# Products of ones ahead of the transposes of norms, two transposes handed on, and keys ahead of relative products, in a decoder kernel of twelve sublayers

## The chip, the cores and the metric

The kernel runs on one core of one Trainium2 chip. The metric is the device time of one execution in microseconds (us); lower is better. The engines are TensorE (PE in the profile, its weight loads PEld), VectorE (DVE), ScalarE (ACT), GpSimd (POOL) and SyncE (SP, which here only issues DMAs). Everything that TensorE multiplies lands in PSUM, eight banks of 128x512 float32 values, and another engine has to take it from there.

## The reference, cut to what matters

A decoder of four layers works on x of 16 sequences x 64 tokens x 128 features. Each layer has three sublayers, and each sublayer ends in the same way:

```
x = layernorm(x + sublayer(x), axis=-1)      # twelve times
```

In order: linear attention (called `la` in the kernel), cross attention to a context (`xa0`), a feed-forward with two layers of local attention and two norms of their own (`lb`); self attention (`at1`), cross attention (`xa1`), a feed-forward (`sf`); a recurrence (`rc`), masked cross attention of 32 heads (`xa2`), a top-1 mixture of 16 experts (`sw`); causal self attention whose scores get q times a table of relative positions (`at3`), cross attention (`xa3`), a top-2 mixture of 8 experts (`tt`). All matrices are float32.

## The kernel before, in words

The 1024 tokens are kept as two halves of 512 (h = 0 and 1), each as four tiles of 128 tokens by 128 features. Between two sublayers a half is held twice: as `xt` (tokens on partitions, for norms and additions) and as `x` (features on partitions, what TensorE needs).

**Norm and flip.** `close` (line 185) ends a sublayer. VectorE makes statistics of y (L195, L197), GpSimd raises the variance to the power -0.5 (L201, L204), VectorE writes `xt` (L206). It returns a function `flip` (line 216), which transposes `xt` with four products on TensorE into a PSUM tile `px` (L222) and has ScalarE copy that out (L224). In `xa0` the flip goes through `shifted` (L233). Between y and the transposes TensorE can do nothing for this half.

**Two streams.** Each half of the sublayers `xa0` to `xa2` is a generator (`first_stream`), and so is each half of `at3` and `xa3` (`second_stream`). `in_turn` (line 1672) chains the sublayers of a half: it starts a sublayer's first part, which for a cross attention are the keys (they need the context alone), before the sublayer ahead of it has flipped. `side_by_side` lets half 0 go 5 steps ahead (2 in the second stream) and then takes a step of each half in turn. Linear attention comes first, without streams: `project_close` (line 252) projects a half, closes it and flips it at once, then does the other half. The expert sublayers `sw` and `tt` run for both halves together, over 23 tiles of 128 rows that are gathered by indirect DMA, computed and written back.

**The order on an engine.** The program order of this Python is not the order on an engine. A planner (the tile framework) takes instructions by their place in the program, but puts a later one first where by its own estimates the earlier one is not ready yet. Tiles come from pools: tag `t` has four PSUM banks of 512 columns and tag `sc` two tiles of two banks (six banks of tag `t` in `sw`, eight in `tt`). A tile's first instruction waits until a buffer is free. What the planner has put into an engine's list is run in that order, and a waiting instruction holds up all that is behind it.

**Products of ones.** `keep_busy` (line 153, its product is L156) multiplies a 128x128 matrix of ones by itself, four times side by side, in bfloat16 into a PSUM tile whose real contents come later, so that its result is never read:

```
self.nc.tensor.matmul(
    out, self.ones_b, self.ones_b.unsqueeze(1).to_broadcast([P, 4, P]), start=True, stop=True
)
```

It needs no data but its PSUM buffer. Before the change such products stand ahead of the projections q and k of each attention (`project`, line 418), two ahead of the scores of an attention without a mask and of the relative products (`scores`, line 461), one ahead of each four transposes of the weights (`turn`, line 539), twelve at the very start and some in `tt`.

**Relative products.** In `at3`, `relative` (line 635) multiplies q by a table (`at_rs`), copies the result to SBUF (`at_rsb`, L651), writes it to DRAM (`at_mem`, L655) and reads it back skewed (`at_rel`, L665): for each half 8 writes and 16 reads, all issued by SP. VectorE adds it to the scores (L527), then come maximum, difference, exponential (L530, L531, L534) and the transposes (L545).

**Local attention.** In each of its two layers `local_half` closes a norm of its own: `hn` (L1007) is transposed into `lb_phn` (L1014), and the first feed-forward products (`lb_pg`, `lb_pa`) follow. The other half's transposes (`lb_pt` L906, `lb_pf` L860) stand between them on TensorE.

**Experts.** At the end of `sw` eight indirect DMAs (L1323) bring each token's row back, VectorE adds each to y (L1450), and both halves are closed and flipped. In `tt` the two gate values go through an exponential (L1494); the first Gelu is in the tile loop (L1569).

Of the kernel before, what the change touches and what calls it, by code (L numbers as in the profile page):

```python
# [11 lines left out]
F32 = mybir.dt.float32  # L12
# [3 lines left out]
AF = mybir.ActivationFunctionType  # L16
# [5 lines left out]
P = 128  # L22
# [15 lines left out]
class Kernel:  # L38
# [143 lines left out]
            nc.vector.tensor_tensor(a, a, rstd, ALU.mult)  # L182
            nc.vector.scalar_tensor_tensor(rstd, a, -3.0, rstd, ALU.add, ALU.mult)

    def close(self, pool, h, y, tag, shift=False):

        nc = self.nc
        stats = self.lnp.tile([P, 4, 6], F32, tag=f"stats{h}", name=f"stats_{tag}{h}")  # L190
        mv = self.lnp.tile([P, 4, 2], F32, tag=f"mv{h}", name=f"mv_{tag}{h}")
        rstd = self.lnp.tile([P, 4], F32, tag=f"rstd{h}", name=f"rstd_{tag}{h}")
        xt = self.xp.tile([P, 4, D], F32, tag=f"xt{h}", name=f"xt_{tag}{h}", bufs=1 + h)
        for i in range(4):
            nc.vector.bn_stats(stats[:, i, :], y[:, i, :])  # L195
        for i in range(4):
            nc.vector.bn_aggr(mv[:, i, :], stats[:, i, :])  # L197
        if tag == "sw":
            self.inverse_deviation(rstd, mv, self.psum(pool, f"pd_{tag}{h}"))
        else:  # L200
            nc.gpsimd.tensor_tensor(  # L201
                rstd, mv[:, :, 1], self.eps.to_broadcast([P, 4]), ALU.add
            )
            nc.gpsimd.tensor_tensor(rstd, rstd, self.minus.to_broadcast([P, 4]), ALU.pow)  # L204
        for i in range(4):
            nc.vector.tensor_scalar(  # L206
                xt[:, i, :], y[:, i, :], mv[:, i, 0:1], rstd[:, i : i + 1], ALU.subtract, ALU.mult
            )
            if tag == "tt":
                at = h * HALF + i * P  # L210
                nc.sync.dma_start(
                    out=self.out.rearrange("b s d -> (b s) d")[at : at + P, :], in_=xt[:, i, :]
                )
        self.xt[h] = xt

        def flip():
            ps = self.psum(pool, f"px_{tag}{h}")
            if shift:
                self.shifted(ps, h, xt)
                return  # L220
            for i in range(4):
                nc.tensor.transpose(ps[:, bass.ts(i, P)], xt[:, i, :], self.g("ident"))  # L222
            x = self.xp.tile([P, HALF], F32, tag=f"x{h}", name=f"x_{tag}{h}")
            nc.scalar.copy(x, ps)  # L224
            self.x[h] = x

        return flip
# [23 lines left out]

    def project_close(self, pool, w, src, bias, tag):

        for h in range(2):
            base = self.base(h, bias, tag)
            ps = self.project(pool, h, w, src, tag)
            y = self.new_y(tag, h)
            self.nc.vector.tensor_tensor(y, ps, base, ALU.add)
            self.close(pool, h, y, tag)()


    def linear_attention(self):


        nc, work, psc, pt = self.nc, self.aw, self.psc, self.pt
        att = self.buf(4, [N], "la_att")
# [93 lines left out]
        for pair in range(4):  # L360
            if pair < 3:
                fronts.append(front(pair + 1))
            back(pair, *fronts[pair])
        self.project_close(pt, self.g("L0a_wo"), att, "L0a_bo", "la")


    @contextmanager
# [36 lines left out]
    def attention(  # L404
        self, h, tag, kv, hd, scale, wq, wk, wv, wo, bq=None, bk=None, bv=None, bo=None,
# [3 lines left out]
        nc = self.nc  # L409
        work, psc, pt = self.aw, self.psc, self.pt  # L410
        x = None
# [5 lines left out]

        def project(name, w, src, b):
            ps = self.psum(pt, f"{tag}_p{name}{h}")
            self.keep_busy(ps)  # L420
            self.group(ps, [(self.g(w), src)])
            t = self.buf(2, [HALF], f"{tag}_{name}{h}")
            if b is None:
                nc.scalar.copy(t, ps)  # L424
            else:
                nc.scalar.activation(t, ps, AF.Identity, bias=self.g(b))
            return t

        def keys(src):

            k = project("k", wk, src, bk)
            kms = []
            for i in range(per):
                if i % 4 == 0:
                    kms.append(self.buf(8, [4, HALF], f"{tag}_km{h}{i}"))
                nc.gpsimd.tensor_scalar(  # L436
                    kms[-1][:, i % 4, :], k, hm[:, i : i + 1], 1.0, ALU.mult, ALU.mult
                )
            return kms
# [21 lines left out]
        def scores(name, q, table, u, gp, local):  # L461

            sc = psc.tile([P, 2, HALF], F32, tag="sc", name=f"{tag}_{name}{h}{u}{gp}")
            masked = name == "sc" and added is not None
            if not masked:
                for gg in range(2):
                    self.keep_busy(sc[:, gg, :])
            for pr in range(many):
                for j in range(2):
                    t = bass.ts((u * many + pr) * 2 + j, S)  # L470
                    for gg in range(2):
                        r = slice(64 * gp + 32 * gg, 64 * gp + 32 * gg + 32)
                        for n, part in enumerate(table):
                            at = pr * width + n * 256
                            nc.tensor.matmul(  # L475
                                sc[64 * j : 64 * j + 64, gg, at : at + 256],
                                q[r, t],
                                part[r, :, t] if local else part[r, :, :],
                                start=not masked or (pr == 0 and n == 0),
                                stop=not masked,  # L480
                                skip_group_check=masked,
                            )
            if masked:
                m = added[:, h * 4 + u * many : h * 4 + (u + 1) * many, :]
                for gg in range(2):
                    nc.tensor.matmul(  # L486
                        sc[:, gg, :],
                        self.ident_b,
                        m.unsqueeze(2).to_broadcast([P, many, per, S]),
                        start=False,  # L490
                        stop=True,
                        skip_group_check=True,
                    )
            return sc


        km = None
        if kv is not None:
            km = keys(kv)
# [8 lines left out]
        steps = [(u, gp) for u in range(units) for gp in range(2)]  # L508
        es, eTs, avs, aos = {}, {}, {}, {}
        q = project("q", wq, x, bq)  # L510
        rels = self.relative(tag, rel, q, h, scores) if rel else None
        km, v = km or keys(x), values()
        y = self.new_y(tag, h) if wo is None else None
        att = None if wo is None else self.buf(2, [HALF], f"{tag}_att{h}")

# [99 lines left out]
        if wo is not None:  # L615
# [11 lines left out]
                    )  # L627
            else:
                nc.vector.tensor_tensor(y, ps, base, ALU.add)
        flip = self.close(pt, h, y, tag, shift=tag == "xa0")  # L630
        yield "last"
        flip()

# [142 lines left out]
    def local_half(self, h):  # L776
# [6 lines left out]
        for l in range(2):  # L783
# [226 lines left out]
                )  # L1010
            yield
            ps = self.psum(pt, f"{tag}_phn")
            for i in range(4):
                nc.tensor.transpose(  # L1014
                    ps[:, bass.ts(i, P)], hn[:, i, :, :].rearrange("p a d -> p (a d)"), ident
                )
# [344 lines left out]
    def switch_ffn(self):  # L1361
        nc, tc, x = self.nc, self.tc, list(self.x)
        E = 16
        with (
# [58 lines left out]
            def second(k, e, hid):  # L1423
# [17 lines left out]
            self.tiles_in_step(  # L1441
                "sw", work, pt, self.sw_in, ids, first, flip, second, between
            )
            back = [one.tile([P, 4, D], F32, name=f"sw_back{h}") for h in range(2)]
            for i in range(8):
                self.gather(back[i // 4][:, i % 4, :], self.sw_out, slot[:, i : i + 1])
            for h in range(2):
                y = self.new_y("sw", h)
                for i in range(4):
                    nc.vector.tensor_tensor(y[:, i, :], base[h][:, i, :], back[h][:, i, :], ALU.add)  # L1450
                self.close(pt, h, y, "sw")()

    def exact_rows(self, src, width, tag):

# [15 lines left out]
    def top2_ffn(self):  # L1470
        nc, tc = self.nc, self.tc
        E = 8
        with (
# [18 lines left out]
            nc.gpsimd.memset(minus, -1.0)  # L1492
            nc.gpsimd.tensor_tensor(m2, m2, m1, ALU.subtract)
            nc.scalar.activation(ex, m2, AF.Exp)  # L1494
            nc.gpsimd.tensor_tensor(w[:, 0, :], ex, self.g("one")[:, 0:8], ALU.add)
            nc.gpsimd.tensor_tensor(w[:, 0, :], w[:, 0, :], minus.to_broadcast([P, 8]), ALU.pow)
            nc.gpsimd.tensor_tensor(w[:, 1, :], ex, w[:, 0, :], ALU.mult)
# [171 lines left out]
                in_=dram["tt_w2"][e : e + 4].rearrange("e (c p) m -> p (e c) m", p=P),  # L1669
            )  # L1670

    def in_turn(self, h, *sublayers):


        parts = [part() for part in sublayers]
        next(parts[0])
        for n, part in enumerate(parts):
            if n + 1 == len(parts):
                yield from part
                break  # L1680
            for ahead in part:
                if ahead == "last":
                    next(parts[n + 1])
                yield

    def first_stream(self, h):
# [4 lines left out]
        def local():  # L1691
            if h == 1:
# [21 lines left out]
                h, "xa2", c, 4, 0.5, "xa2_wq", "xa2_wk", "xa2_wv", "xa2_wo",  # L1714
                "xa2_bq", "xa2_bk", "xa2_bv", "xa2_bo", mask=self.mask_padding,
            ),
        )
        self.score(h, "sw", "sw_wr", 16)
        if h == 0:
# [35 lines left out]

    def run(self, out):
        self.masks, self.rel_table, self.out = {}, None, out
        self.linear_attention()
        self.load("w7")
        self.before = self.keep.tile([P, P], BF16, tag="before", name="before")  # L1760
        self.nc.vector.tensor_scalar(self.before, self.g("count"), self.g("row"), None, ALU.is_gt)
# [209 lines left out]
```

## Time and profile before

| | |
|---|---|
| three runs before | 917.9, 919.42, 914.14 us (median 917.9) |
| the profiled execution | 921.5 us, of which the span from first to last instruction is 919.7 us |
| busy, of the span | PE 80%, PEld 51%, DVE 54%, ACT 39%, POOL 29% |
| granted TensorE clock, mean | 0.858 of full speed |
| the chain that ended last | PE 57%, DVE 20%, POOL 8%, ACT 5%, issue 4%, DMA 3% |

The profile is of one execution. Its page has the busy time of each engine, the span in 40 slices with the granted clock (PEclk, tenths of full speed; 5 is half), and the costliest groups of instructions. The chain of waits is followed back from the last instruction: at each step to what released it. A timeline lists instructions in order of time with start, duration, engine, line, tiles written and read, and in brackets the idle time ahead of the instruction and what ended it. A view of stretches gives the busy time of each engine between two times, and the granted clock there. The names tell the stage: `px_la` is the tile of the flip behind linear attention.

### The profile page before, as it was taken

What the parts mean: (1) busy time and instruction counts of PE and PEld (TensorE: products, weight loads), DVE (VectorE), ACT (ScalarE), POOL (GpSimd) and SP (SyncE); (2) the same over time, 40 slices, a digit from 0 to 9 for tenths busy, and PEclk for the clock granted to TensorE, in tenths of its full rate; (3) what the DMA queues carried; (4) which work ended last, traced back from release to release, by engine and by line L of the source; (5) the groups of instructions that cost most, each with busy time, mean ns of one, the idle gap of its engine ahead of it and who ended that gap; (6) DMA issues with size and microseconds to landing.
All of it is one profiled execution on the core that took longest, in us unless ns stands there. A gap on an engine that the chain in (4) does not pass through costs nothing.

```text
span 919.7 us, 17526 instructions
## 1 busy us (share of the span) xinstructions
PE 737.2 (80%) x7069; PEld 473.0 (51%) x7071; DVE 493.5 (54%) x1126; ACT 360.2 (39%) x599; POOL 264.9 (29%) x299
## 2 busy tenths in 40 slices
PE   7777878778688788889978999769557899957990
PEld 2333546465465455457554577536324565735770
DVE  5554466564836556364437475455434445755663
ACT  2213456354445433364712364333123434512330
POOL 2323133340705321212025300155221111017732
PEclk8766989979989897899976799879867889958995
DMA  8700000000000000500000000232115623031102
GB/s 281 222 1 24 1 1 2 12 1 2 1 1 1 2 1 1 179 6 2 1 1 2 1 2 1 76 101 75 44 54 142 184 73 113 2 115 47 52 27 77
DMA packets 35542, 44.42 MB, mean 48 GB/s; under 512 B 7732, under 2 KB 27445, under 8 KB 34824
## 3 DMA queue, kind: packets, MB, share of 16 engines
q1 hardware_dynamic: 33000, 38.26, 13.4%
q0 software_dynamic: 2464, 5.05, 2.0%
q8 instruction: 57, 0.93, 0.4%
q14 instruction: 21, 0.17, 0.1%
HBM read 34.51 MB, written 11.80 MB: 50 GB/s over the span
## 4 chain that ended last, share of the span: by engine, by line
PE 57%; DVE 20%; POOL 8%; ACT 5%; issue 4%; DMA 3%; SPq 1%; DVEq 0%; POOLq 0%; ACTq 0%
PE xa_sc L475 4%; PE xa_av L566 3%; PE xa_pt L545 3%; PE tt_py L151 3%; PE sw_pe L151 3%; PE tt_ph L151 2%; PE at_pt L545 2%; POOL xa_km L436 2%; DMA at_mem<-at_rsb 2%; PE lb_qk L151 2%; PE lb_pf L860 2%; PE at_av L566 2%; PE xa_sc L486 1%; DVE lb_t L824 1%; DVE lb_t L810 1%
## 5 line engine op out<-in xcount | busy, mean ns | idle before, releaser
L530 DVE TENSOR_REDUCE xa_mx<-xa_sc 128x16 f32<-128x1024 f32 x40 | 48.6, 1218 | 64.9 <-PE xa_sc L486 42.7
L830 POOL TENSOR_TENSOR lb_t<-lb_t,lb_t 128x1024 f32<-128x1024 f32 x16 | 37.7, 2354 | 105.5 <-DVE lb_t L824 88.7
L548 ACT COPY xa_eT<-xa_pt 128x512 f32<-128x512 f32 x80 | 45.5, 587 | 44.2 <-PE xa_pt L545 43.5
L475 PE MATMUL xa_sc<-xa_km,xa_q 32*64 32x256 f32 x640 | 56.4, 404 | 3.6 <-DVE xa_e L531 2.1
L534 ACT ACTIVATE xa_e<-xa_e 128x1024 f32<-128x1024 f32 x40 | 42.3, 1058 | 35.2 <-DVE xa_e L531 35.0
L436 POOL TENSOR_SCALAR xa_km<-xa_k,const 128x512 f32<-128x512 f32 x40 | 27.1, 695 | 92.4 <-ACT xa_k L424 51.7
L545 PE MATMUL xa_pt<-const,xa_e 128*128 128x128 f32 x320 | 50.0, 286 | 2.2 <-ACT xa_e L534 2.2
L531 DVE TENSOR_TENSOR xa_e<-xa_sc,xa_mx 128x1024 f32<-128x1024 f32 x40 | 48.6, 1217 | 2.4 <-ACT xa_eT L548 0.5
L545 PEld LDWEIGHTS xa_pt<-const,xa_e 128*128 128x128 f32 x320 | 41.3, 148 | 14.4 <-ACT xa_e L534 4.5
L566 PEld LDWEIGHTS xa_av<-v,xa_eT 128*64 128x64 f32 x1280 | 40.2, 138 | 7.9 <-issue 6.2
L566 PE MATMUL xa_av<-v,xa_eT 128*64 128x18 f32 (+1 forms) x1280 | 43.7, 209 | 0.0
L151 PE MATMUL lb_qk<-w,lb_hs 128*128 128x512 f32 x64 | 35.2, 675 | 8.9 <-DVE lb_t L824 5.2
L156 PEld LDWEIGHTS <-ones_b 128*128 128x128 bf16 x211 | 21.4, 109 | 35.3 <-issue 21.3
L475 PEld LDWEIGHTS xa_sc<-xa_km,xa_q 32*64 32x64 f32 x640 | 25.2, 137 | 23.0 <-issue 16.1
L806 DVE TENSOR_REDUCE lb_ss<-lb_t 128x16 f32<-128x1024 f32 x16 | 19.5, 1217 | 28.4 <-ACT lb_t L803 28.4
L201 POOL TENSOR_TENSOR rstd_xa<-mv_xa,eps 128x4 f32<-128x4 f32 x8 | 1.6, 201 | 110.3 <-DVE mv_xa L197 110.3
L527 DVE TENSOR_TENSOR at_rel<-at_rel,at_sc 128x1024 f32<-128x1024 f32 x8 | 9.7, 1215 | 40.2 <-PE at_sc L486 23.2
L860 PE MATMUL lb_pf<-const,lb_t 128*128 128x128 f32 x128 | 23.7, 352 | 9.3 <-POOL lb_t L854 7.3
L854 POOL TENSOR_TENSOR lb_t<-lb_t,lb_rs 128x1024 f32<-128x1024 f32 x16 | 30.1, 1899 | 0.0
L156 PE MATMUL xa_pt<-ones_b 128*128 128x512 bf16 x80 | 29.9, 388 | 0.0
L1589 POOL DMA_INDIRECT tt_out<-tt_ys,tt_outs x23 | 22.5, 978 | 19.5 <-DVE tt_ys L1588 16.1
L548 ACT COPY at_eT<-at_pt 128x512 f32<-128x512 f32 x32 | 18.1, 585 | 23.6 <-PE at_pt L545 21.0
(464 smaller groups left out, 1782.7 us busy)
## 6 DMA issues: line engine op xcount, KB each, us to landing
sw_gu<-in_sw_gu SPq DMA_DIRECT2D x4, 1024.0 KB, 7.0
at_mem<-at_rsb SPq DMA_DIRECT2D x16, 256.0 KB, 2.8
at_rel<-at_mem SPq DMA_DIRECT2D x32, 128.0 KB, 3.0
w<-in_w SPq DMA_DIRECT2D x1, 3114.0 KB, 12.1
sw_dn<-in_sw_dn SPq DMA_DIRECT2D x4, 512.0 KB, 6.9
tt_w<-in_tt_w SPq DMA_DIRECT2D x2, 1024.0 KB, 8.4
tt_b<-in_tt_b SPq DMA_DIRECT2D x1, 2048.0 KB, 7.4
sw_in<-in_zeros SPq DMA_DIRECT2D x1, 1472.0 KB, 12.0
```

The lines of the kernel that those rows point to most:

```text
L151: self.nc.tensor.matmul(out, lhsT, rhs, start=n == 0, stop=n == len(pairs) - 1)
L156: self.nc.tensor.matmul(out, self.ones_b, self.ones_b.unsqueeze(1).to_broadcast([P, 4, P]), start=True, stop=True)
L436: nc.gpsimd.tensor_scalar(kms[-1][:, i % 4, :], k, hm[:, i : i + 1], 1.0, ALU.mult, ALU.mult)
L475: nc.tensor.matmul(sc[64 * j : 64 * j + 64, gg, at : at + 256], q[r, t], part[r, :, t] if local else part[r, :, :], start=not masked or (p ...
L530: nc.vector.tensor_reduce(mx, scored, AX.X, ALU.max)
L531: nc.vector.tensor_tensor(e3, scored, mx.unsqueeze(2).to_broadcast([P, 16, S]), ALU.subtract)
L534: nc.scalar.activation(e3, e3, AF.Exp, scale=scale)
L545: nc.tensor.transpose(ps[:, bass.ts(n, P)], blocks[:, bass.ts(n, P)], self.g("ident"))
L548: nc.scalar.copy(eT[:, gg, :], ps)
L566: nc.tensor.matmul(av[64 * j : 64 * j + 64, pr, hp, :, :], eT[:, gg, at : at + 64], v[:, b, hp, :, :], start=True, stop=True,)
L830: nc.gpsimd.tensor_tensor(t1, t1, t2.rearrange("p t n d -> p t (n d)"), ALU.add)
L860: nc.tensor.transpose(ps[:, c, :], t1[:, t, bass.ts(c, P)], ident)
```

## The change

- `close` takes a number `ones`, and `flip` issues that many products of ones into `px` ahead of the transposes: 4 for each half of linear attention, 1 for each half of every attention, but 8 for half 1 of `xa2` and `xa3`, 4 and 2 for the halves of `sw`. The closings of `lb`, `sf`, `rc` and `tt` get none.
- The flips of linear attention are no longer issued by `project_close`: they are returned, and `in_turn` issues each in its half's stream, after the first part (the keys) of `xa0`.
- In `at3`, q and k and the relative products have no products of ones any more (the transposes keep theirs), and k is projected ahead of the relative products, not behind them.
- Each norm in local attention gets six products of ones ahead of the transposes of `hn`.
- At the end of `sw`, each of the four additions to y of half 0 is followed by four float32 products of y with the identity, into a tile that nobody reads.
- In `tt` a Gelu of the exponential's eight values, read by nobody, stands behind that exponential.

```diff
@@ close
-    def close(self, pool, h, y, tag, shift=False):
+    def close(self, pool, h, y, tag, shift=False, ones=0):
...
             ps = self.psum(pool, f"px_{tag}{h}")
+            for _ in range(ones):
+                self.keep_busy(ps)
@@ project_close
-            self.close(pool, h, y, tag)()
+            flips.append(self.close(pool, h, y, tag, ones=4))
+        return flips
@@ attention
             ps = self.psum(pt, f"{tag}_p{name}{h}")
-            self.keep_busy(ps)
+            if not rel:
+                self.keep_busy(ps)
...
-            if not masked:
+            if not masked and not rel:
                 for gg in range(2):
                     self.keep_busy(sc[:, gg, :])
...
         q = project("q", wq, x, bq)
+        km = km or keys(x)
         rels = self.relative(tag, rel, q, h, scores) if rel else None
-        km, v = km or keys(x), values()
+        v = values()
...
-        flip = self.close(pt, h, y, tag, shift=tag == "xa0")
+        ones = 8 if h == 1 and tag in ("xa2", "xa3") else 1
+        flip = self.close(pt, h, y, tag, shift=tag == "xa0", ones=ones)
@@ local_half
             ps = self.psum(pt, f"{tag}_phn")
+            for _ in range(6):
+                self.keep_busy(ps)
@@ switch_ffn
+            busy = self.psum(pt, "sw_busy")
...
+                    if h == 0:
+                        for n in range(4):
+                            nc.tensor.matmul(
+                                busy[:, bass.ts(n, P)], self.g("ident"), y[:, i, :],
+                                start=True, stop=True,
+                            )
-                self.close(pt, h, y, "sw")()
+                self.close(pt, h, y, "sw", ones=4 - 2 * h)()
@@ top2_ffn
             nc.scalar.activation(ex, m2, AF.Exp)
+            ready = one.tile([P, 8], F32, name="tt_ready")
+            nc.scalar.activation(ready, ex, AF.Gelu)
@@ in_turn
         next(parts[0])
+        if flip is not None:
+            flip()
@@ run
-        self.linear_attention()
+        self.flips = self.linear_attention()
```

More of the change, by code (lines that the diff above doesn't have):

```diff
@@ L252, in project_close @@
     def project_close(self, pool, w, src, bias, tag):
+        flips = []
         for h in range(2):
@@ L363, in linear_attention @@
             back(pair, *fronts[pair])
-        self.project_close(pt, self.g("L0a_wo"), att, "L0a_bo", "la")
+        return self.project_close(pt, self.g("L0a_wo"), att, "L0a_bo", "la")
     @contextmanager
@@ L1670, in load_top2, with in_turn @@
             )
-    def in_turn(self, h, *sublayers):
+    def in_turn(self, h, *sublayers, flip=None):
         parts = [part() for part in sublayers]
         next(parts[0])
+        if flip is not None:
+            flip()
         for n, part in enumerate(parts):
@@ L1716, in first_stream @@
             ),
+            flip=self.flips[h],
         )
```

## The prediction

> **What bounds the kernel now.** I read the page first. No engine is full, and the chain that ended last is TensorE for more than half; its clock swings between half and full over the whole span.
>
> ```profile
> PE   7777878778688788889978999769557899957990
> PEclk8766989979989897899976799879867889958995
> PE 57%; DVE 20%; POOL 8%; ACT 5%; issue 4%; DMA 3%; SPq 1%; DVEq 0%; POOLq 0%; ACTq 0%
> ```
>
> Then I asked for the granted clock in short stretches. It is 0.5 or 1.0 and changes only at times that lie multiples of 3.41 us apart (17.10, 23.93, 30.75, 37.58, ...), so I laid the stretches on that grid. Columns: PE, PEld, DVE, ACT, POOL busy, then the clock.
>
> ```profile
> 88.78:92.19 3.41, 3.41 (x16) 2.91 (x15) 2.02 (x2) 1.22 (x3) 0.00 (x0) 0.50 0.00 0
> 92.19:95.61 3.42, 3.42 (x56) 2.40 (x55) 0.33 (x1) 2.04 (x3) 0.00 (x0) 1.00 0.00 0
> 194.59:198.01 3.42, 0.49 (x6) 0.03 (x2) 3.04 (x17) 3.11 (x4) 3.42 (x2) 1.00 0.00 0
> 198.01:201.42 3.41, 1.84 (x9) 1.72 (x10) 2.19 (x4) 0.72 (x2) 1.34 (x2) 0.50 0.00 0
> 201.42:204.83 3.41, 3.41 (x18) 3.41 (x17) 0.00 (x0) 2.47 (x5) 0.00 (x0) 0.50 0.01 2
> 204.83:208.25 3.42, 3.42 (x12) 1.76 (x11) 0.13 (x1) 3.20 (x5) 0.00 (x0) 1.00 0.00 0
> ```
>
> A stretch with little on TensorE (0.49 of 3.41 us) is followed by half clock; full clock comes back only after a stretch full of work. Over all stretches, counting each product by its columns and the share of the 128x128 array that it fills, the clock falls where under about 0.37 of a full-speed stretch was worked, 1.26 us, and returns where about as much was done at half clock. My estimate, from 194 full and 77 half stretches, with 4 exceptions. A product of ones takes 0.21 us at full clock (starts of neighbours), 0.43 at half: six alone make 1.28 us.
>
> The second thing is order. The timeline of TensorE behind linear attention:
>
> ```profile
> 61.65 1.16 PE L151 MATMUL po_la<-w,la_att 128*128 128x128 f32 x8 [0.47 <-ACT la_att L347]
> 66.56 0.48 PE L222 MATMUL px_la<-const,xt_la 128*128 128x128 f32 x1 [3.75 <-DVE xt_la L206]
> 66.83 0.64 PE L151 MATMUL po_la<-w,la_att 128*128 128x128 f32 x2
> ...
> 73.20 0.45 PE L222 MATMUL px_la<-const,xt_la 128*128 128x128 f32 x1 [3.82 <-DVE xt_la L206]
> 73.44 0.63 PE L156 MATMUL xa_pk<-ones_b 128*128 128x512 bf16 x1
> ```
>
> Half 1's projection (`po_la`, second group) had its input since 61.6, yet starts right behind the first transpose of half 0; the keys of `xa0` need the context alone, yet start right behind the first transpose of half 1. I take from this that tiles of a tag get buffers in program order: a tile whose first product waits holds up the next ones. A product of ones as first product takes that hold away.
>
> **Part A, the flips handed on (L222, L151).** Now: norm of half 0, projection of half 1, its norm, then keys. The chain from there:
>
> ```profile
> 72.71 1.12 DVE xt_la L206 x4
> 73.91 1.27 POOL base_xa L680
> 75.17 1.65 issue
> 76.87 2.71 POOL xa_km L436 x4
> 79.58 1.02 POOL mo_m L701
> ```
>
> After: both projections run back to back (61.65 + 1.16 + 1.16 = 64.0), then the keys: one product of ones and two of k, 0.21 + 0.87 at full clock, 1.29 + 0.86 more at half: 65.1 to 66.2. ScalarE's copy 0.69: at most 66.9. GpSimd then has 4 x 0.68 = 2.71 for km, half 1's 1.24 for the norm, 1.02 for the mask: 71.9; the mask's last step 0.44 and the product with it 0.60: first maximum at 72.9. It stands at 81.73: 8.8 saved. If GpSimd puts the base additions first (1.04 + 1.27 per half, 4.6 in all) 4.2 remain. The weights' DMA L128 and the mask's behind it on SP wait for the last `po_la` and move ahead with it. Half 1's flip, now at about 92, adds four products of ones and four transposes, 0.86 + 0.43 = 1.3, where TensorE is busy 12.5 of 13.0 us. Between 2.9 and 7.5; nothing loads GpSimd between 67 and 70 but the first of those additions, so I take **7.0**.
>
> **Part B, six products before hn's transposes, four places.** TensorE sits idle 4.50 us ahead of three of them (195.1 to 199.58 in the first). 1.28 us of ones leave 3.2 us. The clock then holds only if the grid splits the rest so that both neighbouring stretches reach 1.26 us; by the densities on both sides that is about one position in six. In the others the fall comes later, and a stretch of 5.2 us at half clock shrinks to about 3.4. Full clock isn't worth half of 5.8 us (1.15 + 1.71 + 2.98 of `lb_phn`, `lb_pt`, `lb_pf` on the chain): `lb_phn` follows VectorE's `hn` (2.19 for four) and each `lb_pf` needs ScalarE's 0.59 copy, so 1.3 at most. The hold is gone too: `lb_pt`'s input is there at 198.08, 1.5 us before `lb_phn` starts. 0 to 2.8 each; I take 0.9, **3.5** in all. Below nothing: six at half clock, 2.6, still fit the idle time.
>
> A row against a page: in 88.78 to 92.19 fourteen of the sixteen products were transposes, and the clock rose. The Trainium skill (TensorE: Matmul & The Clock Gate, Part 4: PE-mode transpose) says that transposes don't count as activity for the full clock; the trace disagrees. By the page, the flips' own transposes could not hold what the ones gained, and B and C would come to the first rival's sum.
>
> **Part C, eight products for half 1 of xa2 and xa3.** TensorE idles 3.73 us at 590.6 and at 809.1, and the rest runs at half clock: `px_xa` 1.25 against 0.98 at full (576.57), router products 1.89 against 1.06 (578.23). 8 x 0.21 = 1.7, or 3.4 at half, both inside the wait. 1.1 each, in four of five grid positions: **1.8** (0 to 2.2).
>
> **Part D, at3 without ones, keys first.** Half 0: a product at 678.72 and four at 680.80 (0.57 + 1.71 on the chain) go; k's two products (1.71 at half clock) come instead, 0.6 of it under ScalarE's copy of q: 0 to 2, I take 0.5. The table is independent of both. Half 1's product of ones waited for a score buffer, and half 0's transposes behind it:
>
> ```profile
> 699.29 1.06 ACT L534 ACTIVATE at_rel<-at_rel 128x1024 f32<-128x1024 f32 x1 [5.78 <-DVE at_rel L531]
> 702.30 0.59 PE L156 MATMUL at_rs<-ones_b 128*128 128x512 bf16 x1 [3.54 <-DMA at_rel<-at_mem]
> 702.68 1.70 PE L545 MATMUL at_pt<-const,at_rel 128*128 128x128 f32 x7
> ```
>
> Ready at 700.35, started at 702.89: 2.5 lost, all of it before half 1's q and its relative products (708.8). With 0.43, 0.54 and 0.22 of ones on the chain up to there 3.7 at most; the second exponential is held by VectorE's wait for a read, so 3.0. Against: without ones the clock may return a stretch later, 64 relative products at half clock 2.1 longer. Sum -2 to 6; **3.5**.
>
> **Part E, the Gelu ahead.** The load of its table stands on the chain; the next input is ready 0.44 after it starts.
>
> ```profile
> 837.06 0.69 DVE L1568 TENSOR_TENSOR tt_hid<-tt_ph,tt_b 128x512 f32<-128x512 f32 x1
> 837.31 1.28 ACT L1569 ACT_TABLE_LOAD   x1
> ```
>
> 1.28 - 0.44 = **0.8**. At 819.5 ScalarE then idles 4.07 us, which hides the load; a copy or identity in between loads no table in this trace.
>
> **At nothing.** Ten single products in attention flips (0.21 each, in waits where TensorE idles, 16.8 us in all at `px_xa`; without the wait 2 to 4). `sw`: four products per addition, 16 in all, two instructions each of 0.21 at half clock, 6.8 us from 662.95 on; they lie beside a GpSimd-issued gather and end before `xt` (673.15). But from there to q at 679 only 2.2 us of products stand in 9 us, so the clock falls before it pays: 0, at best 2.
>
> **Sum.** 7.0 + 3.5 + 1.8 + 3.5 + 0.8 = 16.6: 921.5 - 16.6 = 904.9 for the profiled execution. The median of the runs is 3.6 lower, 917.9; I predict 917.9 - 16.6 = **901.3**.
>
> **Rivals.**
> 1. The ones change the order but don't hold the clock (the 3.2 us left in B is enough for a fall in five positions of six): A, D, E remain, 11.3: 906.6. For it: the grid. Against: the later fall.
> 2. The gain of A is swallowed, as GpSimd or the single stream's VectorE (6.7 of 10 us at 80 to 90) is late instead: 9.6 remain, 908.3.
> 3. Slower: the planner puts ones ahead of work that is ready, not into waits, at half clock. Off linear attention's first half and `sw` that is 24 + 26 + 4 = 54 products, 23.2 us at 0.43; against A, D, E: 917.9 + 11.9 = 929.8. It decides from about half of them on. Against: at 195, 590 and 809 nothing else was ready. For: the chain shows ones ahead of ready transposes at 702.30.
> 4. Better: the hold's end lets following tiles pass in every norm, B at 8 and D at 6: 894.3 and below.
>
> **How the numbers follow.** Forecast (895 to 904.9) 0.42, rival 1 0.22, rival 2 0.12, rival 4 0.14, rival 3 0.10. The range takes in rivals 1, 2 and 4 with the low ends of A and D: 887 to 913. Half a per cent, 4.6 us, is about what a measurement can tell from no change; faster by it (below 913.3) 0.83, within it 0.08, slower 0.09.
>
> **What would show it.** A: the first `xa_mx` near 73 and `xa_pk` ahead of `px_la`. B: ones at once behind `lb_pv`, `lb_pt` ahead of `lb_phn` or full clock there. C: `tt_pl` near 1.1. D: `at_pt` within 0.1 of its exponential's end near 700. E: no table load at the first Gelu. Wrong if ones stand ahead of ready work in the chain, if `xa_mx` stays near 80, or if the mean clock falls below 0.858.

## The result, and the profile after

The changed kernel takes **892.75 us** (median of 4 runs, 892.14 to 893.58), the kernel before on the same chip 918.66 (4 runs, 914.14 to 927.02): a ratio of **0.971**, with a 95% interval of 0.964 to 0.978. 25.9 us went; 16.6 were forecast, 901.3 us (887 to 913). The time lies in the range, but below the forecast's own band of 895 to 904.9, at rival 4's 894.3 and below. The profiled execution took 892.14 us with a span of 890.4, so 29.3 us less than the profiled one of before; its mean granted clock is 0.893 against 0.858.

The page after; busy time of the engines, the granted clock in 40 slices, and the shares of the chain that ended last:

```profile
PE 737.5 (83%) x7145; PEld 467.7 (53%) x7147; DVE 493.2 (55%) x1126; ACT 361.7 (41%) x602; POOL 264.8 (30%) x299
...
PEclk7878989899999999899977899969968799968995
...
PE 54%; DVE 18%; POOL 7%; ACT 5%; issue 4%; DMA 3%; SPq 1%; DVEq 0%; POOLq 0%; ACTq 0%
```

TensorE has 76 more products and is busy as long as before (737.2 us), so the time went out of its waits; the mean clock says that part of it went out of half clock.

To see where, I cut each span at the same landmarks (starts and ends of named tiles, read from the timelines). Three profiles of the changed kernel stand beside the kernel in which that part is undone. The three come from the first run and from two of the series below; the stretches agree between them within 2.3 us except in `at3` and `tt`.

| stretch, us | before | changed (three profiles) | with the part undone |
|---|---|---|---|
| start to first `po_la` | 61.7 | 62.6, 64.9, 63.3 | |
| to first `xa_mx` | 20.1 | 15.7, 16.2, 16.2 | la_at_once 16.3 |
| to end of last `lb_phn` | 282.8 | 271.2, 272.8, 272.9 | phn1 288.7, phn0 283.3 |
| to last `px_lb` | 20.1 | 21.6, 21.6, 21.6 | phn1 19.7, phn0 20.0 |
| (within these two: first `lb_hn` to last `px_lb`) | 186.6 | 176.6, 177.5, 177.5 | phn1 186.5, phn0 186.1 |
| to last `px_sf` | 116.0 | 114.3, 114.3, 114.3 | no_single 116.0 |
| to last `px_rc` | 19.2 | 17.2, 17.3, 17.2 | no_single 19.2 |
| to last `sw_pl` | 78.4 | 77.5, 77.6, 77.5 | late_undone 78.4 |
| last `sw_back` to last `px_sw` | 8.2 | 8.4, 8.4, 8.3 | late_undone 8.4 |
| `at3`: first q to half 1's x | 97.1 | 87.8, 85.2, 88.4 | relones 95.3, keysback 86.1 |
| to last `tt_pl` | 40.4 | 39.7, 40.8, 40.0 | late_undone 41.0 |
| first `tt_ph` to last `tt_py` | 62.8 | 61.4, 61.6, 71.3 | late_undone 73.1 |

Between the profiles of before and after that is 4.4 us at linear attention, 10.1 in local attention (11.6 less 1.5), 3.7 around `sf` and `rc`, 0.9 at `xa2`, 9.3 in `at3`, 0.7 at `xa3`, 1.4 at the first Gelu: 30.5, less 0.9 for the later start and 0.6 from `sw_pl` to `px_sw`.

The six ones of part B, in the timeline of TensorE after:

```profile
191.64 1.47 PE L156 MATMUL lb_phn<-ones_b 128*128 128x512 bf16 x6
194.76 0.55 PE L914 MATMUL lb_pt<-const,lb_e 128*128 128x128 f32 x3 [1.65 <-ACT lb_e L905]
...
197.26 1.97 PE L868 MATMUL lb_pf<-const,lb_t 128*128 128x128 f32 x16
```

They stand directly behind `lb_pv`'s products, in the wait. `lb_pt` now runs ahead of `lb_phn` (its first transpose starts at 196.11), and sixteen `lb_pf` take 1.97 us where they took 3.19: full clock.

### The profile page after: what moved, and what is told of

Same layout as the page of the kernel before. It is cut to its first block, busy times and chain, and to the rows that moved or that the text cites. A ratio compares the mean times of both kernels' runs of the same rounds, so it can differ in the third digit from the quotient of the medians.

```text
span 890.4 us, 17664 instructions
## 1 busy us (share of the span) xinstructions
PE 737.5 (83%) x7145; PEld 467.7 (53%) x7147; DVE 493.2 (55%) x1126; ACT 361.7 (41%) x602; POOL 264.8 (30%) x299
## 4 chain that ended last, share of the span: by engine, by line
PE 54%; DVE 18%; POOL 7%; ACT 5%; issue 4%; DMA 3%; SPq 1%; DVEq 0%; POOLq 0%; ACTq 0%
PE xa_sc L480 4%; PE xa_av L572 4%; PE xa_pt L551 3%; PE tt_py L151 3%; PE sw_pe L151 3%; PE tt_ph L151 2%; PE at_sc L480 2%; DVE lb_t L818 2%; PE lb_qk L151 2%; DVE lb_t L832 2%; PE at_av L572 2%; PE xa_sc L491 2%; PE at_pt L551 2%; PE xa_pt L156 1%; PE lb_pw L151 1%
## 5 line engine op out<-in xcount | busy, mean ns | idle before, releaser
L554 ACT COPY xa_eT<-xa_pt 128x512 f32<-128x512 f32 x80 | 45.5, 587 | 40.8 <-PE xa_pt L551 40.0
L156 PEld LDWEIGHTS <-ones_b 128*128 128x128 bf16 x255 | 25.3, 106 | 35.9 <-issue 19.8
L1610 POOL DMA_INDIRECT tt_out<-tt_ys,tt_outs x23 | 22.5, 976 | 18.6 <-DVE tt_ys L1609 16.2
L868 PE MATMUL lb_pf<-const,lb_t 128*128 128x128 f32 x128 | 20.1, 312 | 9.4 <-POOL lb_t L862 9.3
L480 PE MATMUL at_sc<-at_km,at_q 32*64 32x256 f32 x256 | 22.5, 446 | 6.0 <-DVE at_rel L533 4.5
L151 PE MATMUL sw_pe<-sw_gu,sw_xs 128*128 x46 | 26.7, 665 | 0.0
## 6 DMA issues: line engine op xcount, KB each, us to landing
w<-in_w SPq DMA_DIRECT2D x1, 3114.0 KB, 13.7
```

What stands on the lines that cost most here:

```text
L151: self.nc.tensor.matmul(out, lhsT, rhs, start=n == 0, stop=n == len(pairs) - 1)
L156: self.nc.tensor.matmul(out, self.ones_b, self.ones_b.unsqueeze(1).to_broadcast([P, 4, P]), start=True, stop=True)
L480: nc.tensor.matmul(sc[64 * j : 64 * j + 64, gg, at : at + 256], q[r, t], part[r, :, t] if local else part[r, :, :], start=not masked or (p ...
L554: nc.scalar.copy(eT[:, gg, :], ps)
```

## The experiments

The runs were made in three series of four, each series on another chip; the kernel before took 935.5 us in the first (phn1, phn0, relones, keysback), 921.5 in the second (after_again, la_at_once, mask_early, no_single) and 933.0 in the third. Times are therefore compared within a series, and across series by stretches. The changed kernel was not run in the first series. At its ratio of 0.971 it would take about 908 us there, an estimate; keysback, which differs from it by the place of the keys alone, took 906.4. The times expected of these four runs were stated for the first chip, so read them as distances from 892.75.

**phn1** and **phn0** (part B: order or clock).

```diff
-            for _ in range(6):
+            for _ in range(1):    # phn0: range(0)
                 self.keep_busy(ps)
```

> The changed kernel with one product of ones ahead of hn's transposes in place of six. Order theory (the first product takes the buffer at once, so lb_pt and lb_pf no longer queue behind lb_phn): one does what six did, 892 to 894, lb_pt still ahead of lb_phn. Clock theory (six are needed to reach the amount that keeps full clock): the 9.9 us that the four norms gained between the landmarks go back, 902 to 903, lb_pf at 3.2 us for sixteen again. I expect something between: the order stays, the clock falls in one to three of the four places, 895 to 900.

> The changed kernel with no product of ones ahead of hn's transposes, as before the change in these four places. Both theories give back the 9.9 us: 902.7 (901 to 904) if the parts are independent. If the clock alone did it, phn1 and this one have the same time; if order alone did it, phn1 stands at 893 and this one at 902.7.

Measured: phn1 916.2 us (912.1 to 925.2), ratio 0.976 (0.969 to 0.983); phn0 913.6 (911.2 to 915.9), 0.975 (0.968 to 0.982); beside keysback's 906.4 they lose 9.8 and 7.2. From the first `po_la` to the last `px_lb` they take 324.6 and 319.9 us; the changed kernel's three profiles take 308.6 to 310.7, keysback and relones, on the same chip, 309.6 and 310.6, before 322.9. Order doesn't do it: with one product `lb_pt` still goes first, and nothing is gained. TensorE in phn1, and then the stretches of the clock's grid there, in phn0 and in the changed kernel (columns: PE, PEld, DVE, ACT, POOL busy with counts, then the clock):

```profile
193.70 0.39 PE L156 MATMUL lb_phn<-ones_b 128*128 128x512 bf16 x1
196.82 0.90 PE L914 MATMUL lb_pt<-const,lb_e 128*128 128x128 f32 x3 [2.73 <-ACT lb_e L905]
198.18 0.47 PE L1024 MATMUL lb_phn<-const,lb_hn 128*128 128x128 f32 x1 [0.46 <-DVE lb_hn L1015]
```

```profile
193.24:196.66 3.42, 0.85 (x7) 0.17 (x3) 3.08 (x16) 3.11 (x4) 3.42 (x2) 1.00 0.00 0
196.66:200.07 3.41, 2.79 (x12) 2.39 (x13) 2.20 (x4) 0.79 (x3) 1.38 (x2) 0.50 0.00 0
```

```profile
190.85:194.27 3.42, 0.78 (x8) 0.25 (x4) 3.15 (x17) 3.12 (x4) 3.42 (x3) 1.00 0.00 0
```

```profile
191.38:194.79 3.41, 1.76 (x11) 0.54 (x7) 3.03 (x14) 3.02 (x4) 3.41 (x3) 1.00 0.00 0
194.79:198.21 3.42, 2.61 (x21) 2.14 (x22) 2.04 (x4) 1.55 (x3) 1.19 (x1) 1.00 0.01 2
198.21:201.62 3.41, 3.41 (x15) 2.04 (x15) 0.00 (x0) 3.39 (x6) 0.00 (x0) 1.00 0.00 0
```

0.85 or 0.78 us of work in a stretch, and the clock falls at its end, for 6.8 us in both; 1.76, and it holds. The sixteen `lb_pf` take 3.54 us in phn1, 3.32 in phn0. Six are enough, one is not; two to five were not run. The 4.8 us by which phn1 is worse than phn0 are lost ahead of these places, where both run the same code: in `xa0` its profile, taken in its 925.2 us run, stays at half clock for 20.48 us from 73.78, phn0's for 6.83 from 78.22. From the first `lb_hn` to the last `px_lb` the two take 186.5 and 186.1 us, before 186.6, the changed kernel 176.6 to 177.5, relones and keysback 177.4 and 175.8. So one is no better than none, not the middle that was expected, and six are worth 9 to 10 us.

**relones** and **keysback** (part D: ones or keys).

```diff
+            self.keep_busy(ps)          # relones: q, k and the relative products
-            if not rel:                 #          with ones again
-                self.keep_busy(ps)
...
-            if not masked and not rel:
+            if not masked:
```
```diff
-        km = km or keys(x)              # keysback
         rels = self.relative(tag, rel, q, h, scores) if rel else None
-        v = values()
+        km, v = km or keys(x), values()
```

> The changed kernel with at3's products of ones put back, the keys still ahead of the relative products. Theory (the ones held half 0's transposes up behind a score buffer): the 9.6 us gained between sw and at3's end go back nearly whole, 900 to 903, at_pt late behind a product of ones again. Rival (the gain is from the keys' place): 892 to 894.

> The changed kernel with at3's keys behind the relative products again, still without ones. Theory (the removed ones gave the gain): 0 to 2 us lost, 893 to 895. Rival (the keys' place gave it): 900 to 903.

Measured: relones 921.7 us (916.5 to 925.6), keysback 906.4 (905.7 to 909.8), in one series. Of the 15.5 us between their two profiles 9.2 lie in `at3`; most of the rest lies at the start (2.7) and in `tt` (2.7), where both run the same code. The removed ones are the gain; the keys' place is worth nothing that shows (86.1 us in `at3`, inside the changed kernel's 85.2 to 88.4). In relones the two ones wait for a score buffer, with half 0's transposes behind them, as in the kernel before:

```profile
692.19 1.01 PE L156 MATMUL at_rs<-ones_b 128*128 128x512 bf16 x2 [1.16 <-DVE at_rel L532]
692.99 1.70 PE L550 MATMUL at_pt<-const,at_rel 128*128 128x128 f32 x7
```

Their exponential had ended at 692.03. In the changed kernel it starts at 679.88 and lasts 1.06, and the transposes follow at once:

```profile
680.13 1.06 PE L156 MATMUL at_pt<-ones_b 128*128 128x512 bf16 x2
680.99 1.97 PE L551 MATMUL at_pt<-const,at_rel 128*128 128x128 f32 x8
```

From the first q, half 1's relative products are copied out after 37.2 us in relones and 39.1 before, 31.5 to 32.2 in the changed kernel: 5 to 7.6 of its gain are order and the ones' own time. The rest comes later, with the clock. relones and before fall for 13.65 us at the fourth of `at3`'s eight exponentials (717.23 and 727.07); phn0, whose `at3` is the changed kernel's, doesn't there. relones first, then phn0:

```profile
713.82:717.23 3.41, 1.78 (x20) 0.66 (x19) 3.41 (x4) 0.06 (x1) 0.00 (x0) 1.00 0.91 292
717.23:720.64 3.41, 2.36 (x10) 2.02 (x11) 3.41 (x5) 2.15 (x3) 0.00 (x0) 0.50 0.81 237
```

```profile
713.10:716.51 3.41, 2.22 (x19) 0.84 (x15) 3.41 (x5) 0.00 (x0) 0.00 (x0) 1.00 0.96 315
716.51:719.92 3.41, 2.23 (x17) 1.91 (x18) 3.41 (x5) 3.31 (x5) 0.00 (x0) 1.00 0.55 151
```

Here 1.78 busy us were too few where 1.76 were enough in local attention: 1.09 of them are score products of 32 by 64, which fill an eighth of the array, and the busy time doesn't show that. Counted as in the prediction (columns times share of the array, an estimate), these 1.78 hold 1.06 us of work, phn0's 2.22 hold 1.32, and the 1.76 of local attention 1.54. This part hangs on the grid. Ten profiles have the changed kernel's `at3`, and behind the copy it takes 52.8 to 60.7 us in them, with 3.4 to 23.9 us of half clock; before takes 58.1 with 17.1. phn1 falls there too and takes 93.4 us for the whole of `at3`. So only the part up to the copy is shown to be the change's own.

**after_again** and **after_third**: the changed kernel as a measure.

> The changed kernel itself, unaltered, as a measure for the others of this series, since the kernel before took 935 where the last four were run and 918 where the changed one was. If all parts scale alike, its ratio to the kernel before is 0.971 again; if the gain is a fixed 26 us, the same within half a per cent.

> The changed kernel once more, as a measure for the three others of this series. From the runs so far: 892 to 898, about 287 to 289 us from the first po_la to half 0's... last lb_phn, 84 to 87 from at3's first q to its last flip.

Measured: 896.3 us (ratio 0.972, 0.968 to 0.977) and 909.3 (0.974, 0.967 to 0.980). The ratio holds on each chip. What differs most between chips is `tt`: from the first `tt_ph` to the last `tt_py` the kernels with the change take 61.2 to 62.0 us in the first run and in the second series, 69.8 to 72.5 in the first and third series (late_undone, without the Gelu, 73.1). Its cause was not looked for.

**la_at_once** (part A).

```diff
-            flips.append(self.close(pool, h, y, tag, ones=4))
-        return flips
+            self.close(pool, h, y, tag, ones=4)()
+        return None
...
-            flip=self.flips[h],
+            flip=None,
```

> The changed kernel with linear attention's transposes issued at once again behind each norm (the four products of ones stay), so the keys of xa0 stand behind half 1's norm. Theory (A gave 3.4 at the first xa_mx): 3.4 us over the changed kernel, first xa_mx near 82. Rival (A gave its 7.0 and lost some of it later): 6 to 7 us over it. Third case: nothing of it reaches the end, as later stages wait for something else: 0.

Measured: 898.1 us (887.3 to 898.7) beside after_again's 896.3 (892.6 to 898.5): not told apart. The first `xa_mx` stands 16.3 us behind `po_la`, as with the flips handed on (15.7 to 16.2), not 20.1. TensorE there:

```profile
62.73 1.03 PE L156 MATMUL px_la<-ones_b 128*128 128x512 bf16 x4
63.59 1.05 PE L151 MATMUL po_la<-w,la_att 128*128 128x128 f32 x8
...
65.35 0.38 PE L156 MATMUL xa_pk<-ones_b 128*128 128x512 bf16 x1
67.36 0.33 PE L224 MATMUL px_la<-const,xt_la 128*128 128x128 f32 x1 [1.63 <-DVE xt_la L206]
```

Half 1's projection passes half 0's flip because ones take the flip's buffer. Up to this landmark la_at_once differs from the kernel before by the four ones of each half alone, and with them 20.1 becomes 16.3: handing the flips on as well adds nothing that shows. Whether handing on would do it without the ones was not run. It brings the keys 2.8 us earlier (`xa_pk`'s product stands at 67.5 here, at 64.7 in the changed kernel), but they don't end last.

**mask_early**, **mask_mid**, **mask_mid_at_once** (what ends last in A). GpSimd in the changed kernel:

```profile
74.97 1.26 POOL L688 TENSOR_TENSOR base_xa<-base_xa,xt_la 128x512 f32<-128x512 f32 x1 [1.23 <-DVE xt_la L206]
76.19 1.04 POOL L709 TENSOR_TENSOR mo_m<-mo_m,cols 128x512 f32<-128x512 f32 x1
```

The mask stands behind an addition that waits for half 1's norm; TensorE idles 3.40 us ahead of the product with it, which starts at 77.74. The two later profiles idle only 1.88 and 1.89 us there, as q's two products ran at half clock (2.08 against 1.12), and that is the most that an earlier mask could bring in them. Three kernels make the mask sooner:

```diff
+        self.masks["xa0"] = self.mask_outer(self.aw)   # mask_early, in run
         self.flips = self.linear_attention()
...
                 fronts.append(front(pair + 1))
+            else:                                      # mask_mid, in linear_attention
+                self.masks["xa0"] = self.mask_outer(work)
             back(pair, *fronts[pair])
```

> The changed kernel with xa0's mask made ahead of linear attention instead of behind half 1's norm. Theory (A's missing 3.5 us went to mo_m, which stands behind half 1's norm and the second base addition in GpSimd's list): the first xa_mx comes 3 to 3.5 us earlier beside its own po_la (at 16 us less than now behind it 13), and the time falls by about 3 us. Rival (VectorE and the scores are as late themselves): under 1 us.

> The changed kernel with xa0's mask made ahead of linear attention's last pair, where SP and GpSimd have room, so that nothing ahead of the first po_la waits for it (made ahead of the whole, it moved the first po_la from 62 to 79). Theory: from po_la to the last lb_phn the 284.5 of mask_early against 287 to 289 of the changed kernel, here without the 16 us of delay: 2.5 to 4.5 us faster than the changed kernel. Rival: mo_m's place costs linear attention as much as it saves: 0 to 1.

> As mask_mid, and linear attention's transposes issued at once behind each norm. Without the mask's move that left the time as it was (16.3 us from po_la to the first xa_mx, 284.3 to the last lb_phn). Theory (handing the flips on helps once the mask is out of the way, as the keys then come 2.8 us earlier): 1 to 3 us slower than mask_mid. Rival (handing them on costs, as half 1's eight instructions lie in a busy stretch): the same or 1 to 3 us faster than mask_mid.

Measured: 905.8 us (900.0 to 906.3) beside 896.3; 912.0 (905.5 to 915.0) and 912.1 (908.0 to 920.2) beside 909.3. The first `xa_mx` stands 15.0, 14.8 and 17.3 us behind `po_la`: the mask was worth about 1 us in that stretch, not 3.5. What is late next in mask_mid is q: VectorE's four `xt_la` take 3.07 us, the clock falls at 75.61 while TensorE waits for them, and q's two products take 2.08 at half clock instead of 1.12. mask_early also moves the first `po_la` to 79.0: its mask waits in GpSimd's list for a transfer behind SP's first loads (31.38), and GpSimd's `la_sq` of linear attention, at 19.08 in the changed kernel, comes at 35.34. In mask_mid the first `po_la` stands at 69.1, in mask_mid_at_once, with the same mask, at 62.8; whether the mask delays it is not shown. Between these two the handed-on flips are worth 2.5 us at the landmark (17.3 against 14.8), but 1.2 of them is that the first scores and the product with the mask ran at half clock in the one profile (2.95 against 1.74). Both kernels of mask_mid lose 3.3 us at `px_rc` again (20.5 and 20.6 against 17.2), where the clock stays at half for 10.2 us instead of 3.4. No version here beats the changed kernel.

**no_single** (the ten single ones).

```diff
-        ones = 8 if h == 1 and tag in ("xa2", "xa3") else 1
+        ones = 8 if h == 1 and tag in ("xa2", "xa3") else 0
```

> The changed kernel without the single product of ones ahead of the attention stages' transposes (the eights of xa2 and xa3 stay). By the prediction 0, at best 2 lost. Theory from the traces: the 4 us that the stretch between px_sf and px_rc of half 1 gained come from them (the hold of buffers is gone, or the clock): 3 to 5 us over the changed kernel. Rival (the 4 us come from how the clock's grid lay in the one run of before): 0 to 1.

Measured: 896.7 us (892.8 to 899.0) beside 896.3: not told apart. By stretches they are worth 3.7 us, in the two around `sf` and `rc`, which go back to 116.0 and 19.2 to the tenth. The changed kernel there, then no_single:

```profile
484.92:488.33 3.41, 3.41 (x22) 2.72 (x24) 2.81 (x4) 2.21 (x4) 0.91 (x1) 0.50 0.02 5
488.33:491.74 3.41, 3.41 (x19) 1.46 (x14) 2.48 (x3) 1.27 (x3) 0.00 (x0) 1.00 0.00 0
```

```profile
483.26:486.67 3.41, 3.41 (x21) 2.60 (x23) 2.02 (x3) 1.92 (x4) 0.78 (x1) 0.50 0.02 5
486.67:490.08 3.41, 3.41 (x12) 0.87 (x6) 2.60 (x4) 0.69 (x1) 0.00 (x0) 0.50 0.00 0
```

Half clock lasts one stretch in the first and three in the second (to 493.50), for nearly the same products. Counted as in the prediction (an estimate), the first of these stretches holds 1.30 us of work in the changed kernel and 1.22 in no_single, on the two sides of its 1.26: a small shift against the grid goes with it (`px_sf` ends 0.59 and 2.25 us behind a grid point). The 3.7 don't show in the times.

**late_undone** (C, `sw`, E).

```diff
-        ones = 8 if h == 1 and tag in ("xa2", "xa3") else 1
+        ones = 1
...
-                    if h == 0:
-                        for n in range(4):
...
-                self.close(pt, h, y, "sw", ones=4 - 2 * h)()
+                self.close(pt, h, y, "sw")()
...
-            nc.scalar.activation(ready, ex, AF.Gelu)
```

> The changed kernel with three late parts undone, each read in its own stretch: one product of ones in place of eight ahead of half 1's transposes in xa2 and xa3 (C), no products in sw's additions and none ahead of its transposes, no Gelu ahead in tt (E). By the stretches so far: C 0.9 us between px_rc and the last sw_pl (77.5 to 78.4) and 0 to 1 at tt_pl; sw's products 0 (8.4 against 8.2); E 1.2 between the first tt_ph and the last tt_py (62.8 against 61.4). Sum 2 to 3 us slower than the changed kernel. Rival (single ones do what eight do, and the eights' gain was the grid): 1 to 1.5, E alone.

Measured: 910.6 us (907.6 to 921.1) beside after_third's 909.3 (908.7 to 910.9): not told apart. By stretches: C 0.9 at `xa2`; at `xa3` 41.0 against 39.7 to 40.8, no more than profiles of the same code differ; `sw`'s products 0 (8.4 against 8.3); E 1.8 (73.1 against 71.3, where the two other kernels of the series, with the Gelu, take 70.5 and 72.0). Part C shows in the router's products: `sw_pl` of half 1 takes 1.07 us in the changed kernel's three profiles, 1.89 here and before. `tt_pl` of half 1 takes 1.06, 1.88 and 1.29, 1.88 here and before: at `xa3` the eights keep full clock in one profile of three. ScalarE in the changed kernel:

```profile
791.66 1.28 ACT L1515 ACT_TABLE_LOAD   x1
```

The load has moved into a wait. In late_undone it stands at 817.28, and the first Gelu starts behind it, at 818.58. From the end of the first `tt_hid` to its Gelu pass 0.85 us before, 2.31 in late_undone and 0.03 in the changed kernel's three profiles. Other kernels with the load moved take 0.03 to 1.59, so the time in late_undone isn't the load's alone.

## Why the prediction was right, and where its sizes were off

Direction held, and B, D and E worked at the places that they named, C at one of its two, A by another step than the one that it was derived from. The total was 9.3 us short, and the terms' errors have both signs: A and C gave less than forecast, the single ones gave more in the stretches, and B and D each gave almost three times their term. That the time still fell into the range owes something to its width and to A and C falling short.

- **A, 7.0 forecast, 3.9 to 4.4 measured.** The hold of the flip's buffer is real, and ones remove it. But the step that set the first maximum at 72.9 put the mask behind half 1's norm only; it stands behind half 1's base addition as well, at 76.19. The prediction had priced GpSimd's additions ahead at 4.2 and set that aside for 7.0. The mask alone is worth about 1 us, because `xt_la`, and with it q, is late beside it (3.07 us, which no term had). By its own signs the part comes out badly: `xa_mx` was to stand near 73, and near 80 was to be wrong; it stands at 78.4, 81.0 and 79.4, of which 1.0 to 3.2 is a later start. Handing the flips on, from which I derived the part, gave nothing that shows.
- **B, 3.5 forecast, 9 to 10 measured** (176.6 to 177.5 us against 186.1 in phn0). The failed step is "about one position in six": I took the program's place on the grid as drawn at random. It isn't (below). In the first profile the clock held in the first, second and fourth place and fell for one stretch in the third (300.60); in all eleven profiles with six ones it holds in the second and fourth and falls for one stretch in the third. The other failed step is the 1.3 at most for a held clock: read at the work that follows each place, the four gave 2.7, 2.8, 1.3 and 3.1 us, and the 1.3 is the place where the clock fell.
- **C, 1.8 forecast, 0.9 and about nothing measured.** Right at `xa2`; at `xa3` full clock held in one profile of three, where four in five were counted on.
- **D, 3.5 forecast, 9 measured (8.7 to 11.9 in three profiles, 3.7 to 12.4 in all ten with this `at3`).** The mechanism at 702.30 is right (its row of transposes starts at 702.68, so 2.3 us were lost there, not 2.5); 3.0 up to half 1's relative products was 5 to 7.6. The 2.1 us set against it, half clock lasting longer without ones, did not come: half 1's relative products ran at full clock in all three profiles. What lies behind them is the clock's grid, and no step had it; of the 17.1 us at half clock before, 6.8 to 13.7 are left in the three profiles, 23.9 in two of the ten.
- **E, 0.8 forecast, 0.8 measured at the first Gelu** (0.85 less 0.03). Right; the 1.2 to 1.8 of the whole stretch are little more than profiles of the same code differ.
- **At nothing.** `sw`'s products are worth nothing, as forecast. The single ones are worth 3.7 us in the stretches, where "at best 2" was too low, and nothing that shows in the times (896.7 against 896.3).
- **The rivals.** Rival 1, ones that don't hold the clock, fell with phn1. Rival 2 came half true: about 3 of A's 7.0 were swallowed by GpSimd and VectorE, but at 67 to 77 us, not in the 80 to 90 that it named for VectorE. Rival 3 did not occur: the ones stand in waits. Rival 4's time (894.3 and below) came true with another mechanism: B and D did give more than 8 and 6, but tiles that pass, without the clock, gave nothing in phn1.

The row against the page held again. In 194.79 to 198.21 of the changed kernel all 21 products that TensorE ran are transposes, and the clock stayed full behind them. The Trainium skill (TensorE: Matmul & The Clock Gate, Part 4: PE-mode transpose) would have had it fall there.

## What to carry to other kernels

Read the granted clock on its own grid of 3.41 us and count the work in each stretch. In the waits of 4.5 us here six products of ones kept the clock, and one was no better than none. A product of ones as first writer of a buffer lets later tiles pass, but one that itself waits for a buffer holds up ready work. Before crediting a change of order, undo it alone: here four ones made the gain that the handed-on flips were meant to bring. Before calling a difference between two profiles the edit's, look where it begins: phn1 lost its 4.8 us ahead of the edit.

## What the runs showed of the hardware that was not expected

**The program locks onto the clock's grid.** The grid lies anywhere when the program starts: TensorE's first product comes 0.47 to 3.26 us behind a grid point in the fourteen profiles. At the first `po_la` they still stand 0.04 to 3.38 us behind one. At the end of the last `lb_phn` it is 1.08 to 1.21 us in all eleven with six ones (2.88, 2.96 and 2.65 in phn0, phn1 and before), at the last `px_lb` 1.96 to 2.38 in all fourteen, and stretches repeat to 0.1 us between chips (114.3 and 17.2 in the table). A likely reason, argued and not shown: where the clock rises within work, a program that is late by some time is late by half of it afterwards; where it falls within a wait nothing is added. So behind local attention an edit's place on the grid was the same in every profile here, and a small edit ahead of it can move it: both kernels of mask_mid lie 0.4 us earlier at `px_sf` (0.14 and 0.25 behind a grid point, 0.49 to 0.66 in the others that have the single ones) and stay at half clock three times as long.

**VectorE waits for GpSimd, instruction by instruction.** Half 0's four `xt_la` took 3.07 us beside GpSimd's base addition (1.05) and `km` (0.68 each), half 1's 1.11 alone; each of the four ends 0.08 us behind a GpSimd instruction. In la_at_once only the first has GpSimd beside it: it takes 1.06, the others 0.33 to 0.34. The transposes that wait for them start 0.67 apart:

```profile
68.24 0.33 PE L224 MATMUL px_la<-const,xt_la 128*128 128x128 f32 x1 [1.42 <-DVE xt_la L206]
68.91 0.33 PE L224 MATMUL px_la<-const,xt_la 128*128 128x128 f32 x1 [0.34 <-DVE xt_la L206]
```

The Trainium skill (SBUF — State Buffer, Who interferes with whom) states that GpSimd and VectorE share a pair of ports under an exclusive lock, which some VectorE instructions (`tensor_scalar`, as here, among them) can need for the whole instruction; a pace of 0.67 beside instructions of 0.68 agrees.
